# A pairwise bilinear kernel: five equal x tiles in a ring, w first, fewer places ahead, and one more block of x through GpSimd

## The chip, the cores and the metric

The kernel runs on one core of one Trainium2 chip. The metric is the device time of one execution in microseconds (us). All executions that are compared here are in the fast state. One kernel varies by 1 to 5 us from run to run, so the experiments were run in five rounds beside the kernel before on the same chip, and they come with a 95% interval.

## The reference

For every pair i < j of the 32 features of a row, the feature vector x[i] (64 numbers) is multiplied by the pair's own 64 x 64 matrix, and the product is multiplied by x[j] element by element.

```python
def _L0_rec_ref(inputs, W):                      # inputs (4096, 32, 64), W (496, 64, 64)
    idx_i, idx_j = np.triu_indices(F, k=1)       # 496 pairs
    vi = inputs[:, idx_i, :]
    vj = inputs[:, idx_j, :]
    vidots = jnp.einsum('bpd,pde->bpe', vi, W)
    return vidots * vj                           # (4096, 496, 64) float32
```

The output is 520 MB, the inputs are 42 MB. The kernel mainly writes.

## The kernel before

The rows are worked on in 32 tiles of 128 rows, two tiles to a block. For each tile TensorE turns x (a transpose), multiplies by w, and VectorE multiplies the product by x[j] on its way out of PSUM. Some steps (`aside`) go through ScalarE and GpSimd instead. A finished group of pairs, about 4 MB, is stored from one of three buffers in `ob`. The names PE, DVE, ACT, POOL and SP in the profile are TensorE, VectorE, ScalarE, GpSimd and the queue that issues the stores. In the code, `...` marks what is left out; type annotations are left out too.

```python
    LEAD = 3                        # the first three tiles run side by side, group by group
    # ring of five x tiles; blocks in slots 0 and 3 have a gap of 16 numbers between their tiles
    starts = [0, FD + GAP, 2 * FD + GAP, 3 * FD + GAP, 4 * FD + 2 * GAP]
    def slot_of(blk):
        e, second = divmod(blk, 2)
        return ((1, 3), (2, 0))[e % 2][second]

    SWR = 120
    def turn_engines(k):            # a tiny transfer: which engines GpSimd's next transfer begins on
        ...
    def load_fifteen(blk):          # a block of x on GpSimd's queue, for 15 engines of 16
        rows = rows_of(x, blk).rearrange("(p k) f d -> p k f d", k=NB)
        dst = x_block(blk)
        def part(ps, ks):
            tc.keep_in_program_order(nc.gpsimd.dma_start(out=dst[ps, ks], in_=rows[ps, ks]))
        part(slice(0, SWR), slice(0, NB))
        turn_engines(1)
        for k in range(NB):
            part(slice(SWR, P), slice(k, k + 1))
    ...
    AHEAD = 6                       # x is turned so many steps before its first use
    LATE = 4                        # two blocks are loaded in the 5th step of every 4th tile
    loads = {place[2 * NB * e - 1, LATE]: 2 * e for e in range(1, NBLK // 2)}

    load_x(0, nc.sync, 0, 1)        # start: half a block of x, then w
    load_w(0)
    load_w(1)
    ...
    for s, (t, st) in enumerate(sched):
        if s in loads:
            load_fifteen(loads[s] + 1)                          # odd block: GpSimd
        if s - 3 in loads:
            tc.keep_in_program_order(load_x(loads[s - 3], nc.scalar))   # even block: ACT
        ...                                                     # turns, matmuls
        if i in aside and c0 == 0:
            nc.scalar.copy(dst, src)
            nc.gpsimd.tensor_mul(dst, dst, xj)
        else:
            nc.vector.tensor_mul(dst, src, xj)
        if pa + m in ends:
            nc.sync.dma_start(out=..., in_=ot[...])             # store of a group
```

Of the kernel before, what the change touches and what calls it, by code (L numbers as in the profile page):

```python
# [8 lines left out]
F32 = mybir.dt.float32  # L9
# [3 lines left out]
def kernel(  # L13
# [17 lines left out]
    nc = tc.nc  # L31

    B, F, D = x.shape
    P = 128
    NB = 2
    assert 2 * D == P and B % (2 * NB * P) == 0
    NBLK = B // (NB * P)
    NT = NBLK * NB
# [4 lines left out]
    RUN = 8  # L43
# [9 lines left out]
    LEAD = 3  # L53
# [3 lines left out]
    for t in range(NT):  # L57
        b = lead if t < LEAD else later
# [4 lines left out]
    const = ctx.enter_context(tc.tile_pool(name="const", bufs=1))  # L63
# [4 lines left out]

    wT = const.tile([P, NP, E2], F32, tag="wT", name="wT")
    FD = F * D  # L70
    GAP = 16
    xb = const.tile([P, 5 * FD + 3 * GAP], F32, tag="xb", name="xb")
    XT = 2 * (RUN // 2) * P
    xtb = const.tile([P, 2 * XT], F32, tag="xtb", name="xtb")
    ob = const.tile([P, 3 * cap1, D], F32, tag="ob", name="ob")
# [4 lines left out]
    def out_home(n: int, later_: bool):  # L80
        o, c = ((2 - n % 3) * cap1, cap1) if later_ else ((2 - n % 3) * cap0, cap0)
        return ob[:, o : o + c, :]
# [8 lines left out]
    def xt_home(t: int):  # L91
        n = xt_used[0]
        xt_used[0] += 1
        n = n % 4 if t < LEAD else n % 2
        mem, o = (xtb, n * XT) if n < 2 else (xb, (n - 2) * XT)
        return mem[:, o : o + XT].rearrange("p (s u b) -> p s u b", s=2, b=P)





    starts = [0, FD + GAP, 2 * FD + GAP, 3 * FD + GAP, 4 * FD + 2 * GAP]

    def slot_of(blk: int):
        e, second = divmod(blk, 2)
        return ((1, 3), (2, 0))[e % 2][second]

    def tile_of(t: int):

        blk, k = divmod(t, NB)  # L110
        return blk, 1 - k if slot_of(blk) == 0 else k

    def x_block(blk: int):
        o = starts[slot_of(blk)]
        step = starts[slot_of(blk) + 1] - o
        wide = xb[:, o : o + NB * step].rearrange("p (k n) -> p k n", k=NB)
        return wide[:, :, :FD].rearrange("p k (f d) -> p k f d", d=D)

    def x_tile(t: int):
        blk, k = tile_of(t)  # L120
        return x_block(blk)[:, k]

    def rows_of(dram: bass.AP, blk: int) -> bass.AP:
        return dram[blk * NB * P : (blk + 1) * NB * P]

    def load_x(blk: int, eng, k0: int = 0, k1: int = NB):
        src = rows_of(x, blk).rearrange("(p k) f d -> p k f d", k=NB)
        return eng.dma_start(out=x_block(blk)[:, k0:k1], in_=src[:, k0:k1])
# [4 lines left out]
    SWR = 120  # L133
# [4 lines left out]
    def turn_engines(k: int):  # L138
        n = k if k > 1 else 17
        c = used[0] % 8  # L140
        used[0] += 1
        src = x[: NB * n].rearrange("(p k) f d -> p k f d", k=NB)
        tc.keep_in_program_order(
            nc.gpsimd.dma_start(out=scratch[:n, :, c : c + 1], in_=src[:, :, 0, 0:1])  # L144
        )

    def load_fifteen(blk: int):
        rows = rows_of(x, blk).rearrange("(p k) f d -> p k f d", k=NB)
        dst = x_block(blk)

        def part(ps: slice, ks: slice):
            tc.keep_in_program_order(nc.gpsimd.dma_start(out=dst[ps, ks], in_=rows[ps, ks]))  # L152

        part(slice(0, SWR), slice(0, NB))
        turn_engines(1)
        for k in range(NB):
            part(slice(SWR, P), slice(k, k + 1))



# [4 lines left out]
    def raw_w(c: int):  # L165
        if c + 1 < len(wrows):
            a = wrows[c + 1][0]
            return wT[:, a : a + P, :].rearrange("p r e -> p (r e)")
        return ob[:, 3 * cap1 - RAW :, :].rearrange("p r e -> p (r e)")

    def load_w(c: int):
        a = wrows[c][0]
        nc.sync.dma_start(out=raw_w(c), in_=wflat[a : a + P])

    def order_w(c: int, k: int, copy):

        r = wrows[c][1] - wrows[c][0]
        o = k * RP if c == 0 else 3 * cap1 - RAW - (1 + k % 2) * RP
        rp = ob[:, o : o + RP, :].rearrange("p r e -> p (r e)").rearrange("p (e h d) -> p e h d", h=2, d=D)
        src = raw_w(c)[:r].rearrange("p (d h e) -> p e h d", h=2, d=D)  # L180
        ins = copy(rp[:r], src[:, k * EU : (k + 1) * EU])  # L181
        if c > 0:
            tc.keep_in_program_order(ins)
        return rp

    def turn_w(c: int, k: int, rp, copy):
        a, b = wrows[c]
        r = b - a
        pt = psum.tile([P, EU, P], F32, tag="ps", name=f"ptw_{c}_{k}")
        for n in range(EU):  # L190
            nc.tensor.transpose(pt[:, n, :r], rp[:r, n].rearrange("p h d -> p (h d)"), ident[:r, :r])  # L191
        copy(wT[:, a:b, k * EU : (k + 1) * EU], pt[:, :, :r].rearrange("p e r -> p r e"))  # L192

    def turn_x(t: int, q: int, copy):


        pt = psum.tile([P, RUN // 2, P], F32, tag="ps", name=f"ptx_{t}_{q}")
        for u in range(RUN // 2):
            f = q * RUN + 2 * u
            nc.tensor.transpose(pt[:, u, :], x_tile(t)[:, f : f + 2, :].rearrange("p f d -> p (f d)"), ident)  # L200
        xT = xt_home(t)
        copy(xT[:, 0], pt)  # L202
        copy(xT[D:, 1], pt[:D])  # L203
        copy(xT[:D, 1], pt[D:])  # L204
        return xT
# [15 lines left out]
    first = {}  # L221
# [13 lines left out]
    place = {ts: n for n, ts in enumerate(sched)}  # L235


    AHEAD = 6
    due: dict = {}
    for t in range(NT):  # L240
        for q in range(F // RUN):
            at = place[t, first[t, q * RUN]] - AHEAD
            due.setdefault(max(0, at), []).append(("x", t, q))
    for c, orders, turns in (
        (1, (2, 4, 8, 10), (4, 7, 12, 15)),
# [6 lines left out]
    LATE = 4  # L252
    loads = {place[2 * NB * e - 1, LATE]: 2 * e for e in range(1, NBLK // 2)}

    load_x(0, nc.sync, 0, 1)
    load_w(0)
    load_w(1)
    load_x(0, nc.sync, 1, NB)
    load_x(1, nc.sync)
# [3 lines left out]

    v, p, a = nc.vector.tensor_copy, nc.gpsimd.tensor_copy, nc.scalar.copy
    xT, rps = {}, {}
    xT[0, 0] = turn_x(0, 0, a)
    due[0] = [d for d in due[0] if d != ("x", 0, 0)]
    for k, copy in enumerate((v, v, v, a)):
        rps[0, k] = order_w(0, k, copy)
    for k, copy in ((0, a), (3, a), (1, v), (2, a)):  # L270
        turn_w(0, k, rps.pop((0, k)), copy)

    n_out = {}
    for s, (t, st) in enumerate(sched):
        blk, kt = tile_of(t)
        g, i, c0, m = steps[t][st]
        if s in loads:
            load_fifteen(loads[s] + 1)
        if s - 3 in loads:
            tc.keep_in_program_order(load_x(loads[s - 3], nc.scalar))  # L280
        for what, *args in due.get(s, ()):
            if what == "x":
                xT[tuple(args)] = turn_x(*args, a)
            elif what == "turn":
                turn_w(*args, rps.pop(tuple(args)), a)
            else:
                c, k = args
                rps[c, k] = order_w(c, k, ((v, v, p, v), (v, v, p, a))[k % 2][c])

        base, end = groups[t][g]  # L290
        pa = p0[i] + c0
        if pa == base:
            ot = out_home(len(n_out), t >= LEAD)
            n_out[t, g] = ot
        ot = n_out[t, g]
        ps = psum.tile([P, 2, CH, E2], F32, tag="ps", name=f"ps_{s}")
        for h in range(2):
            nc.tensor.matmul(  # L298
                ps[:, h, :m, :],
                xT[t, i // RUN][h * D : (h + 1) * D, (i + h) % 2, i % RUN // 2, :],  # L300
                wT[h * D : (h + 1) * D, pa : pa + m, :],
                start=True,
                stop=True,
            )
        o = pa - base
        j = i + 1 + c0
        dst = ot[:, o : o + m, :].rearrange("p m (h e) -> p m h e", h=2)
        src = ps[:, :, :m, :].rearrange("p h m e -> p m h e")
        xj = x_tile(t)[:, j : j + m, :].rearrange("p m (h e) -> p m h e", h=2)
# [6 lines that stand above are left out]
        ends = (p0[2], end) if (t, g) == (0, 0) else (end,)  # L316
        if pa + m in ends:
            n0 = p0[2] if len(ends) > 1 and pa + m == end else base
            nc.sync.dma_start(
                out=rows_of(out, blk).rearrange("(p k) n d -> p k n d", k=NB)[:, kt, n0 : pa + m, :],  # L320
                in_=ot[:, n0 - base : pa + m - base, :],
            )
# [28 lines left out]
```

## Time and profile before

| | before |
|---|---|
| time | 1334.1 us (median of 3 runs) |
| profiled span | 1333.2 us |
| busy: PE, DVE, ACT, POOL | 86%, 71%, 35%, 42% |
| moved by DMA | 563.16 MB, 422 GB/s over the span |

A row of the page's second part has 40 slices of the span; a digit is a busy share in tenths. In a line of the waits the first engine waits and the one behind the arrow is what it waited for. In a line of the windows come the times, then busy time (and instructions) of PE, PEld, DVE, ACT and POOL, the granted clock, the DMA share and GB/s. A DMA share of 1.00 means that all 16 engines had packets in hand, and 0.06 that one had. A share of 1.00 at a low rate means packets that take longer than usual.

### The profile page before, as it was taken

The numbers are of one execution on the slowest core, as the hardware profiler recorded it, in microseconds if no ns is written. First come the engines' busy times: TensorE is split into PE (matmuls) and PEld (weight loads), VectorE is DVE, ScalarE is ACT, GpSimd is POOL, SyncE is SP. The second block draws the span as 40 slices with busy tenths as digits, with TensorE's granted clock in tenths as the row PEclk, the third lists the DMA queues.
The fourth block names the chain that finished last, engine by engine and source line by source line (L and its number), as shares of the span: only waits on it lengthen the run. The fifth ranks groups of instructions, "written<-read, shape, count | busy, mean of one in ns | idle before, by whom it ended". The sixth has DMA issues, their size and how long they took to land.

```text
span 1333.2 us, 17377 instructions
## 1 busy us (share of the span) xinstructions
PE 1146.3 (86%) x6644; PEld 597.9 (45%) x6644; DVE 952.0 (71%) x1287; ACT 471.6 (35%) x627; POOL 558.5 (42%) x264
## 2 busy tenths in 40 slices
PE   6989989996989979998888888888888988888983
PEld 3555444443444434444444444444444444444441
DVE  5778767875777757777667776777767776677773
ACT  4553423333333323333233332343333332333330
POOL 1862524435434434344344352444434444334440
PEclk9999989998999989999899998999989999899997
DMA  9999999999999999999999999999999999999997
GB/s 389 431 430 429 381 428 433 429 433 422 428 431 434 426 423 431 430 431 428 420 435 428 434 411 426 428 433 430 422 425 437 424 430 403 428 433 430 424 426 307
DMA packets 24306, 563.16 MB, mean 422 GB/s; under 512 B 3232, under 2 KB 3232, under 8 KB 3360
## 3 DMA queue, kind: packets, MB, share of 16 engines
q1 hardware_dynamic: 20576, 532.69, 93.5%
q0 software_dynamic: 2640, 14.70, 2.8%
q10 hardware_dynamic: 1008, 14.68, 2.8%
q8 instruction: 52, 0.85, 0.2%
q14 instruction: 30, 0.25, 0.0%
HBM read 41.94 MB, written 520.09 MB: 422 GB/s over the span
## 4 chain that ended last, share of the span: by engine, by line
DMA 48%; PE 25%; DVE 11%; issue 8%; POOL 4%; ACT 3%; DVEq 0%; SPq 0%; ACTq 0%; POOLq 0%
DMA out_dram<-ob 47%; PE ps L298 22%; DVE ob L314 11%; POOL ob L312 3%; ACT ob L311 2%; PE ptx L200 2%; DMA xb<-in_r_inputs_dram 1%; PE ptw L191 1%; POOL xb L152 0%; DVE ob L181 0%; POOL scratch L144 0%; POOL ob L181 0%; DVEq L314 0%; ACT xtb L202 0%; ACT xtb L204 0%
## 5 line engine op out<-in xcount | busy, mean ns | idle before, releaser
L314 DVE TENSOR_TENSOR ob<-ps,xb 128x1024 f32<-128x1024 f32 (+4 forms) x1277 | 939.8, 793 | 347.9 <-DMA out_dram<-ob 173.8
L298 PE MATMUL ps<-wT,xtb 64*128 64x512 f32 (+15 forms) x5760 | 1015.4, 490 | 145.9 <-DVE ob L314 72.5
L312 POOL TENSOR_TENSOR ob<-ob,xb 128x1024 f32<-128x1024 f32 x224 | 529.1, 2367 | 744.6 <-ACT ob L311 717.3
L298 PEld LDWEIGHTS ps<-wT,xtb 64*128 64x128 f32 x5760 | 507.6, 195 | 619.2 <-DVE ob L314 257.1
L311 ACT COPY ob<-ps 128x1024 f32<-128x1024 f32 x224 | 226.8, 1013 | 485.9 <-PE ps L298 342.5
L202 ACT COPY xtb<-ptx 128x512 f32<-128x512 f32 x122 | 71.5, 586 | 311.4 <-PE ptx L200 309.7
L200 PE MATMUL ptx<-ident,xb 128*128 128x128 f32 x512 | 86.2, 292 | 10.8 <-DMA xb<-in_r_inputs_dram 7.1
L200 PEld LDWEIGHTS ptx<-ident,xb 128*128 128x128 f32 x512 | 55.1, 144 | 61.9 <-issue 37.5
L204 ACT COPY xtb<-ptx 64x512 f32<-64x512 f32 x122 | 71.0, 582 | 3.0
L203 ACT COPY xtb<-ptx 64x512 f32<-64x512 f32 x122 | 70.4, 577 | 2.9
L298 PE MATMUL ps<-wT,xb 64*128 64x512 f32 (+15 forms) x244 | 42.5, 465 | 3.4 <-DVE ob L314 1.6
L298 PEld LDWEIGHTS ps<-wT,xb 64*128 64x128 f32 x244 | 20.2, 185 | 21.3 <-DVE ob L314 9.4
L191 PE MATMUL ptw<-ident,ob 128*128 128x128 f32 (+1 forms) x128 | 18.1, 294 | 6.0 <-DVE ob L181 5.8
L191 PEld LDWEIGHTS ptw<-ident,ob 128*128 128x128 f32 (+1 forms) x128 | 15.1, 154 | 12.0 <-DVE ob L181 5.2
L192 ACT COPY wT<-ptw 128x1024 f32<-128x1024 f32 (+1 forms) x15 | 14.9, 992 | 10.1 <-PE ptw L191 10.0
L181 DVE COPY ob<-wT 128x1024 f32<-128x1024 f32 (+1 forms) x7 | 9.5, 1382 | 10.5 <-DMA wT<-in_L_rec_W_dram 10.5
L152 POOL DMA_DIRECT2D xb<-in_r_inputs_dram x21 | 13.3, 636 | 0.0
L202 ACT COPY xb<-ptx 128x512 f32<-128x512 f32 x6 | 3.5, 586 | 18.1 <-PE ptx L200 18.1
L144 POOL DMA_DIRECT2D scratch<-in_r_inputs_dram x9 | 8.4, 934 | 0.3 <-issue 0.3
L181 POOL COPY ob<-wT 128x1024 f32<-128x1024 f32 x4 | 8.0, 2004 | 0.0
L181 ACT COPY ob<-ob 128x1024 f32<-128x1024 f32 x2 | 4.1, 2028 | 0.0
L204 ACT COPY xb<-ptx 64x512 f32<-64x512 f32 x6 | 3.5, 583 | 0.1
(11 smaller groups left out, 11.3 us busy)
## 6 DMA issues: line engine op xcount, KB each, us to landing
out_dram<-ob SPq DMA_DIRECT2D x29, 4064.0 KB, 19.5
out_dram<-ob SPq DMA_DIRECT2D x29, 4032.0 KB, 19.9
out_dram<-ob SPq DMA_DIRECT2D x29, 4000.0 KB, 19.8
out_dram<-ob SPq DMA_DIRECT2D x29, 3776.0 KB, 20.2
xb<-in_r_inputs_dram ACTq DMA_DIRECT2D x7, 2048.0 KB, 22.5
xb<-in_r_inputs_dram POOLq DMA_DIRECT2D x7, 1920.0 KB, 33.7
out_dram<-ob SPq DMA_DIRECT2D x3, 2912.0 KB, 12.6
out_dram<-ob SPq DMA_DIRECT2D x3, 2624.0 KB, 11.2
```

Of the source, the lines that this page charges most:

```text
L152: tc.keep_in_program_order(nc.gpsimd.dma_start(out=dst[ps, ks], in_=rows[ps, ks]))
L181: ins = copy(rp[:r], src[:, k * EU : (k + 1) * EU])
L191: nc.tensor.transpose(pt[:, n, :r], rp[:r, n].rearrange("p h d -> p (h d)"), ident[:r, :r])
L192: copy(wT[:, a:b, k * EU : (k + 1) * EU], pt[:, :, :r].rearrange("p e r -> p r e"))
L200: nc.tensor.transpose(pt[:, u, :], x_tile(t)[:, f : f + 2, :].rearrange("p f d -> p (f d)"), ident)
L202: copy(xT[:, 0], pt)
L203: copy(xT[D:, 1], pt[:D])
L204: copy(xT[:D, 1], pt[D:])
L298: nc.tensor.matmul(ps[:, h, :m, :], xT[t, i // RUN][h * D : (h + 1) * D, (i + h) % 2, i % RUN // 2, :], wT[h * D : (h + 1) * D, pa : pa + ...
L311: nc.scalar.copy(dst, src)
L312: nc.gpsimd.tensor_mul(dst, dst, xj)
L314: nc.vector.tensor_mul(dst, src, xj)
```

## The change

The intent was to make the five tiles of the ring equal (no gap) and put the two tiles of a GpSimd block into places that don't touch; to have w's first part and the first matmuls sooner; and to give block 14, too, to GpSimd, whose loads leave one DMA engine out.

```diff
-    GAP = 16
-    xb = const.tile([P, 5 * FD + 3 * GAP], F32, tag="xb", name="xb")
+    xb = const.tile([P, 5, FD], F32, tag="xb", name="xb")
...
+    fifteen = (3, 5, 7, 9, 11, 13, 14, 15)
+    def slots_of(blk: int):
         e, second = divmod(blk, 2)
-        return ((1, 3), (2, 0))[e % 2][second]
+        if e == 0:
+            return ((1, 2), (3, 4))[second]
+        if e % 2 == 0:
+            return ((2, 3), (1, 4))[second]
+        if 2 * e in fifteen:
+            return ((1, 3), (2, 0))[second]
+        return ((1, 2), (3, 0))[second]
...
-        part(slice(0, SWR), slice(0, NB))
+        part(slice(0, SWR), slice(0, F))
         turn_engines(1)
-        for k in range(NB):
-            part(slice(SWR, P), slice(k, k + 1))
+        for h in range(2):
+            part(slice(SWR, P), slice(h * F // 2, (h + 1) * F // 2))
...
-    AHEAD = 6
+    AHEAD = {t: 4 if t < LEAD else 6 for t in range(NT)}
...
+    load_w(0)
     load_x(0, nc.sync, 0, 1)
-    load_w(0)
...
-    xT[0, 0] = turn_x(0, 0, a)              # now after two of the four turns of w
...
         if s in loads:
-            load_fifteen(loads[s] + 1)
-        if s - 3 in loads:
+            for b in (loads[s], loads[s] + 1):
+                if b in fifteen:
+                    load_fifteen(b)
+        if s - 3 in loads and loads[s - 3] not in fifteen:
```

The last 8 rows of a GpSimd block thus come in halves by features (16 pieces of 4 KB each) and no longer by tiles (8 pieces of 8 KB each).

More of the change, by code (lines that the diff above doesn't have):

```diff
@@ L94, in xt_home @@
         n = n % 4 if t < LEAD else n % 2
-        mem, o = (xtb, n * XT) if n < 2 else (xb, (n - 2) * XT)
+        mem, o = (xtb, n * XT) if n < 2 else (xb[:, 0], (n - 2) * XT)
         return mem[:, o : o + XT].rearrange("p (s u b) -> p s u b", s=2, b=P)
-    starts = [0, FD + GAP, 2 * FD + GAP, 3 * FD + GAP, 4 * FD + 2 * GAP]
-    def slot_of(blk: int):
+    fifteen = (3, 5, 7, 9, 11, 13, 14, 15)
+    def slots_of(blk: int):
         e, second = divmod(blk, 2)
-        return ((1, 3), (2, 0))[e % 2][second]
+        if e == 0:
[5 more added lines that the diff above has]
+        return ((1, 2), (3, 0))[second]
     def tile_of(t: int):
         blk, k = divmod(t, NB)
-        return blk, 1 - k if slot_of(blk) == 0 else k
+        a, b = slots_of(blk)
+        return blk, k if a < b else 1 - k
     def x_block(blk: int):
-        o = starts[slot_of(blk)]
-        step = starts[slot_of(blk) + 1] - o
-        wide = xb[:, o : o + NB * step].rearrange("p (k n) -> p k n", k=NB)
-        return wide[:, :, :FD].rearrange("p k (f d) -> p k f d", d=D)
+        a, b = sorted(slots_of(blk))
+        return xb[:, a : b + 1 : b - a].rearrange("p k (f d) -> p k f d", d=D)
     def x_tile(t: int):
@@ L149, in load_fifteen, with part @@
         dst = x_block(blk)
-        def part(ps: slice, ks: slice):
-            tc.keep_in_program_order(nc.gpsimd.dma_start(out=dst[ps, ks], in_=rows[ps, ks]))
-        part(slice(0, SWR), slice(0, NB))
+        def part(ps: slice, fs: slice):
+            tc.keep_in_program_order(nc.gpsimd.dma_start(out=dst[ps, :, fs], in_=rows[ps, :, fs]))
+        part(slice(0, SWR), slice(0, F))
         turn_engines(1)
-        for k in range(NB):
-            part(slice(SWR, P), slice(k, k + 1))
+        for h in range(2):
+            part(slice(SWR, P), slice(h * F // 2, (h + 1) * F // 2))
     wflat = w.rearrange("p d e -> p (d e)")
@@ L241 @@
         for q in range(F // RUN):
-            at = place[t, first[t, q * RUN]] - AHEAD
+            at = place[t, first[t, q * RUN]] - AHEAD[t]
             due.setdefault(max(0, at), []).append(("x", t, q))
@@ L271 @@
         turn_w(0, k, rps.pop((0, k)), copy)
+        if k == 3:
+            xT[0, 0] = turn_x(0, 0, a)
     n_out = {}
```

## The prediction

> **What bounds the kernel now.** I read four things in this order: the rates by slice and the queues on the page, windows of two microseconds at the end, the waits, and the timeline around one load of x.
>
> The page first: the mean busy share of the 16 DMA engines in 40 slices, what they moved, and the queues.
> ```profile
> DMA  9999999999999999999999999999999999999997
> GB/s 389 431 430 429 381 428 433 429 433 422 428 431 434 426 423 431 430 431 428 420 435 428 434 411 426 428 433 430 422 425 437 424 430 403 428 433 430 424 426 307
> ...
> q1 hardware_dynamic: 20576, 532.69, 93.5%
> q0 software_dynamic: 2640, 14.70, 2.8%
> q10 hardware_dynamic: 1008, 14.68, 2.8%
> q8 instruction: 52, 0.85, 0.2%
> ```
> The engines are busy nearly all the time and the rate has a plateau at 428 to 437 GB/s. The kernel is DMA-bound: the queues' shares add to 99.3%. PE (86%) and DVE (71%) follow. So shortening a chain of arithmetic pays only where a DMA engine would have had nothing to do. The rate is low in four places: the first slice (2 us before the first packet), slice 5 (381), the slices with a load of x (403 and 411 the worst) and the last (307).
>
> The last slice, in windows of 2 us. The last two columns are DMA share and GB/s; nothing computes any more.
> ```profile
> 1322.00:1324.00 2.00, 0.00 (x0) 0.00 (x0) 0.00 (x0) 0.00 (x0) 0.00 (x0) 0.50 0.75 323
> 1324.00:1326.00 2.00, 0.00 (x0) 0.00 (x0) 0.00 (x0) 0.00 (x0) 0.00 (x0) 0.50 0.08 32
> 1326.00:1328.00 2.00, 0.00 (x0) 0.00 (x0) 0.00 (x0) 0.00 (x0) 0.00 (x0) 0.50 0.04 16
> 1328.00:1330.00 2.00, 0.00 (x0) 0.00 (x0) 0.00 (x0) 0.00 (x0) 0.00 (x0) 0.50 0.07 32
> ```
> A share of about 1/16 means that one engine is still working, 8 us after the rest. The trace also holds each transfer's 16 landing times, one per engine. For the last store they are 1323.89 (first), 1323.99 (8th), 1325.4 (15th) and 1332.13 (last). **One DMA engine, always behind, sets the end.** The distance from 8th to last is 1.3 us for the store issued at 313.16, after two loads of x, and grows to 8.1 for the last store before the load at 790 and to 9.1 before that at 1116. After these two loads it is 2.6 and 4.7, then it grows to 8.15 at the end.
>
> Why it lags: queue 8 (instructions) has 52 packets of 16 KB. In the trace one comes about every 25 us, they never overlap, and they take 950 ns on average: 49.5 us. I infer that they are all on this engine; the trace doesn't name engines. Why the lag drops: GpSimd's loads give 120 rows to 15 engines and leave one out.
>
> Now the waits: first the store queue's own, then DVE's on a buffer of ob.
> ```profile
> SPq L319 <- DVE ob L314: 1133.9, 135, 19.3
> ```
> ```profile
> DVE ob L314 <- DMA out_dram<-ob: 173.8, 77, 8.2
> ```
> The store queue waits for DVE with two stores usually outstanding (19.5 us to landing, about 9.4 us each), so this costs nothing while the queue is stocked. DVE's wait is for the slow engine: a buffer is free only when its last engine has landed.
>
> Last the start, in windows of the columns PE, PEld, DVE, ACT, POOL, clock, share, GB/s.
> ```profile
> 120.00:138.00 18.00, 17.34 (x128) 10.22 (x124) 15.74 (x30) 4.77 (x9) 0.00 (x0) 1.00 0.99 423
> 138.00:156.00 18.00, 17.93 (x110) 9.63 (x110) 15.77 (x22) 7.29 (x9) 12.77 (x9) 1.00 0.98 354
> 156.00:172.00 16.00, 9.59 (x60) 4.83 (x56) 6.96 (x12) 5.52 (x8) 6.47 (x3) 0.90 1.00 418
> ```
> Until 156 us PE is 96 to 100% busy and just fails to keep the queue stocked: the store issued at 139.49 came as its predecessor's first share landed (139.48); the next, at 150.46, came after the first landing of that one (147.94), and its first packets ran only at 155. Against 432 GB/s, 138 to 156 lost (432 - 354) x 18 / 432 = 3.3 us.
>
> **What the Trainium skill says.** "DMA: Bandwidth & Descriptors", section "Where 436 GB/s comes from", gives a ceiling of 435 GB/s for 16 ports. The trace agrees: a store packet of 32512 B takes 1204 ns, 27.0 GB/s, or 432 on 16. Its section "Why a DMA increments its semaphore by 16 and not by 1" says that all 16 engines must report, and that GpSimd's transfers on fewer engines go to consecutive ones from a rotating cursor. The first agrees with the landing times above; the second fits the falls of the lag but no view names an engine. Section "Queues, rings and completion order" says that an engine takes its queues in turn, a packet each. The trace agrees: beside stores of 30 KB packets GpSimd's 8 KB ones move about 92 GB/s (321 to 330 us).
>
> **The change part by part.**
>
> *Block 14 moves from ACT to GpSimd.* On ACT's queue the slow engine gets 8 packets of 16 KB, 8 x 611 = 4.89 us. Of GpSimd's load it gets 1 packet of 8 KB, 0.31 us. It saves 4.58 us. The 15 others go from 4.89 to 17 x 309 ns = 5.25 us, +0.36 each. During the load at 1116 the slow engine's landings of two successive stores are 1121.48 and 1135.87, 14.4 us apart, which is just 8 store packets of 1.194 us and 4.89 us of x: it ran without a hole, so the saving comes through whole: its end moves from 1332.13 to 1327.55, and the others' last from 1325.4 to 1325.8. It remains last.
>
> What that load costs on GpSimd: issuing one block took 0.83 + 1.01 + 1.07 = 2.91 us, and it sits between two multiplies that the first store of that tile needs:
> ```profile
> 1116.53 0.83 POOL L152 DMA_DIRECT2D xb<-in_r_inputs_dram  x1
> 1117.36 1.01 POOL L144 DMA_DIRECT2D scratch<-in_r_inputs_dram  x1
> ...
> 1118.36 1.07 POOL L152 DMA_DIRECT2D xb<-in_r_inputs_dram  x2
> ...
> 1119.44 2.36 POOL L312 TENSOR_TENSOR ob<-ob,xb 128x1024 f32<-128x1024 f32 x1
> ```
> Its store went out at 1121.83. With two blocks it goes 2.9 us later. For 15 engines that is a longer time without stores, but they have 3.9 MB of GpSimd's loads to do then; the slow one has stores left until about 1131. Block 14 then moves at 92 GB/s instead of sharing with ACT: first packet some 4.7 us after issue, 1.97 MB / 92 = 21.4 us, and about 2.2 us for each of three small transfers behind. It is whole at about 1149, against 1139 on ACT. Tile 28 was first turned at 1153. This just fits.
>
> *w first.* 1 MB of x took 2.45 us of the queue (first share of w landed 4.9 us after it for 2 MB), so w lands at 8.0 instead of 10.5. The w turns end some 2 us earlier with the x turn among them. *Four places ahead.* Tile 1's turn stood before the first matmul of tile 0 and waited for x until 17.86; now two steps (about 1 us of PE each) go before it. Together PE's work from 18 to 156 us moves forward by about 2 us. The loads already fill the DMA until 33, so nothing is gained there; at 138 to 156 the stores come 2 us sooner. The slow engine took 18.2 us from 152.07 to 170.29 for some 13.4 us of packets, so part of these 2 us is also its own. I choose 1.2.
>
> *Five equal tiles, blocks apart, halves by features.* GpSimd's odd blocks were already in 8 KB packets (a gap of 64 B kept them apart). The same packets go to other tiles; the two small parts become 4 KB pieces in the same number of bytes. Block 1 gets 16 KB packets in place of 8 KB: 16 x 309 - 8 x 611 = 0.06 us. Zero.
>
> Sum: 1334.1 - 4.6 - 1.2 = 1328.3; a little for the later store at 1125: 1328.5.
>
> **Rivals.** (a) The loads take longer, not shorter. GpSimd's queue alone with 3.9 MB could hold tile 28 past 1153. For: the small transfers land 2.2 us apart. Against: the queue holds one to two stores (9.4 us each). If it stalls by over 8 us: 1332 to 1336. (b) The 15 others become the bound, because the later store starves them: they have only 1.8 us of room. A hole of 3 us makes 1329 to 1330. (c) The new places interleave two blocks, so the program might take the strided ranges as overlapping and make ACT's load wait for GpSimd's (34 us to landing) six times. For: ACT works in order, so its copies would stall behind. Against: the strides describe disjoint tiles. It would be 1360 or more. (d) The start gains all of 3.3 us for all engines: 1326. (e) The spared engine is not the slow one: then -0.8, 1333. The falls of the lag speak against it.
>
> **Range and chances.** Nearly all ways lie within 0.7% of before; the bytes don't change. The largest gain that I can make of the tail and the start is 8 us, 0.6%; 2% would be 27 us. Only (c) makes over 2% slower. Range 1325 to 1333.
>
> **What would show it.** Right: the last store's last landing is some 3 us behind its 8th instead of 8.1; one fewer ACT load of x and 2 more small GpSimd transfers; the first store goes out 1.5 to 3 us before 25.24; slice 5 is above 390 GB/s; the mean rate rises from 422 to 424 GB/s (563.16 MB in some 1327.6 us). Wrong: the tail still ends with one engine alone for 8 us; waits on x appear in PE's list beyond the 7.1 us at the start; or ACT's x loads are issued tens of microseconds after GpSimd's.

## The result, and the profile after

The changed kernel took 1330.03 us (median of 4 runs, 1329.89 to 1332.44), the kernel before beside it 1334.9 us (4 runs). The ratio is 0.9966 (0.9949 to 0.9984). A ratio here is the mean time of one kernel's fast runs over that of the other's of the same rounds, so it isn't quite the ratio of the medians. The profiled span is 1328.1 us.

First the page after, its rates by slice and its queues:

```profile
GB/s 388 432 429 432 384 429 434 430 431 424 431 429 435 431 412 432 430 430 431 422 432 427 431 417 419 434 429 432 414 427 431 430 431 382 419 432 431 430 431 387
...
q1 hardware_dynamic: 20448, 532.69, 93.8%
q0 software_dynamic: 3264, 16.80, 3.5%
q10 hardware_dynamic: 864, 12.58, 2.4%
q8 instruction: 52, 0.85, 0.2%
```

One block of 2.1 MB has gone from queue 10 (ACT) to queue 0 (GpSimd). The last slice has 387 GB/s instead of 307. Slice 5 (133 to 166 us) has hardly moved, 384 against 381. And a new low has come up: 382 in slice 34, where block 14 is loaded, against 403.

The end after, in windows of 2 us:

```profile
1320.00:1322.00 2.00, 0.00 (x0) 0.00 (x0) 0.00 (x0) 0.00 (x0) 0.00 (x0) 0.50 0.90 387
1322.00:1324.00 2.00, 0.00 (x0) 0.00 (x0) 0.00 (x0) 0.00 (x0) 0.00 (x0) 0.50 0.97 419
1324.00:1326.00 2.00, 0.00 (x0) 0.00 (x0) 0.00 (x0) 0.00 (x0) 0.00 (x0) 0.50 0.38 161
1326.00:1328.00 2.00, 0.00 (x0) 0.00 (x0) 0.00 (x0) 0.00 (x0) 0.00 (x0) 0.50 0.00 0
```

The 6.8 us in which one engine worked alone (from the 15th landing at 1325.38 to the last at 1332.13) are gone: all 16 end within 3 us. But the others now work at full share until 1324, later than before. The 16 landing times of a store, which the trace holds without the engines' names, show both (in us):

```
store                    kernel     first     8th      15th     last
issued 1101.3 / 1100.6   before    1112.25  1112.38  1116.28  1121.48
                         after     1111.52  1112.40  1114.44  1120.19
(load of blocks 14, 15)
issued 1147.6 / 1141.2   before    1161.72  1162.64  1164.48  1167.33
                         after     1159.60  1164.82  1165.25  1165.99
the last store           before    1323.89  1323.99  1325.38  1332.13
                         after     1324.10  1325.54  1326.59  1326.95
```

In front of that load the last landing comes 1.3 us earlier than before, and the 8th at the same time. Behind it the last landing is one of the crowd, and the 8th comes 2.2 us later than before. In the changed kernel it is the *first* landing that moves: 5.2 us ahead of the 8th after the load, 1.1 us ahead in the store issued at 1271. That is the movement which the *last* one makes before (4.7 us behind the 8th after the load, 8.1 at the end).

The packets show that it is the same engine. Each of the 8 packets that a store gives an engine starts within 6 ns of the end of the one before, so an engine's work can be followed by its times. In the kernel before, the 40 packets from 1263.7 to 1312.5 us that lead to the last landing took 44 ns more, on the mean, than the least for their size; the other engines' packets in that time took 8 ns more. Packets of 32000 B, for instance, took 1213 to 1265 ns on it and 1189 (median) on the others. In the changed kernel the engine with this mark is the first to land at 1159.60. It then falls back into the crowd and is fifth in the last store, at 1324.97. So it lost its place as last, and led at first.

What happened in the load. GpSimd's timeline after, which answers to the one that the prediction shows:

```profile
1113.53 2.36 POOL L319 TENSOR_TENSOR ob<-ob,xb 128x1024 f32<-128x1024 f32 x1 [12.97 <-ACT ob L318]
1115.83 0.79 POOL L156 DMA_DIRECT2D xb<-in_r_inputs_dram  x1
1116.61 0.98 POOL L148 DMA_DIRECT2D scratch<-in_r_inputs_dram  x1
1117.59 1.86 POOL L156 DMA_DIRECT2D xb<-in_r_inputs_dram  x3
1119.45 0.96 POOL L148 DMA_DIRECT2D scratch<-in_r_inputs_dram  x1
1120.41 1.10 POOL L156 DMA_DIRECT2D xb<-in_r_inputs_dram  x2
1121.54 6.99 POOL L319 TENSOR_TENSOR ob<-ob,xb 128x1024 f32<-128x1024 f32 x3
```

GpSimd issues for 5.7 us, and only then come the multiplies for which the store of this tile waits; it goes out at 1123.93, and 1121.83 before. The windows of this stretch, before and then after:

```profile
1110.00:1120.00 10.00, 9.96 (x56) 4.76 (x54) 7.05 (x10) 3.01 (x4) 5.75 (x6) 1.00 1.01 424
1120.00:1130.00 10.00, 7.11 (x32) 3.77 (x34) 6.18 (x7) 2.79 (x4) 5.23 (x3) 0.83 0.97 352
```
```profile
1110.00:1120.00 10.00, 9.26 (x48) 4.21 (x44) 6.35 (x7) 3.69 (x5) 6.47 (x7) 1.00 1.06 436
1120.00:1130.00 10.00, 7.29 (x44) 3.99 (x44) 7.13 (x8) 2.10 (x3) 8.50 (x6) 1.00 0.94 253
```

For ten microseconds the rate is 253 GB/s at a share of 0.94: the 15 engines have almost only GpSimd's loads, and these packets of 8 KB take longer (a median of 614 ns) than the 309 ns that they need elsewhere.

The start. DVE's and ACT's waits for a buffer of `ob` between 24 and 66 us, before and then after:

```profile
ACT ob L311 <- DMA out_dram<-ob: 2.6, 2, 2.1
...
DVE ob L314 <- DMA out_dram<-ob: 1.7, 1, 1.7
```
```profile
DVE ob L321 <- DMA out_dram<-ob: 8.7, 3, 4.1
...
ACT ob L318 <- DMA out_dram<-ob: 5.8, 2, 3.0
```

The first matmul on w begins at 17.13 instead of 18.56 us and the third store goes out at 34.18 instead of 37.05. But then the engines wait 14.5 us for buffers instead of 4.3, and by the eleventh store (85.27 against 85.57) the lead is 0.3 us.

### The profile page after: what moved, and what is told of

Same layout as the page of the kernel before. It is cut to its first block, busy times and chain, and to the rows that moved or that the text cites. A ratio compares the mean times of both kernels' runs of the same rounds, so it can differ in the third digit from the quotient of the medians.

```text
span 1328.1 us, 17383 instructions
## 1 busy us (share of the span) xinstructions
PE 1142.9 (86%) x6644; PEld 599.4 (45%) x6644; DVE 950.6 (72%) x1287; ACT 471.1 (35%) x627; POOL 561.5 (42%) x268
## 4 chain that ended last, share of the span: by engine, by line
DMA 49%; PE 22%; DVE 11%; issue 9%; POOL 4%; ACT 3%; DVEq 0%; ACTq 0%; SPq 0%; POOLq 0%
DMA out_dram<-ob 48%; PE ps L305 20%; DVE ob L321 10%; POOL ob L319 3%; ACT ob L318 3%; PE ptx L204 2%; DMA xb<-in_r_inputs_dram 1%; POOL xb L156 0%; ACT xtb L206 0%; ACT xtb L208 0%; ACT xtb L207 0%; DVE ob L185 0%; PE ptw L195 0%; POOL ob L185 0%; ACT ob L185 0%
```

## The experiments

| run | what it is | us (median) | ratio to before, 95% |
|---|---|---|---|
| changed kernel | | 1330.03 | 0.9966 (0.9949 to 0.9984) |
| e1_act14 | changed, block 14 on ACT | 1333.34 | 0.9986 (0.9979 to 0.9992) |
| e2_old_start | changed, old start | 1330.76 | 0.9959 (0.9946 to 0.9971) |
| e3_before_whole | before, blocks 13 and 15 on all 16 engines | 1339.86 | 1.0033 (1.0021 to 1.0045) |
| e4_after_whole15 | changed, block 15 on all 16 engines | 1332.40 | 0.9971 (0.9960 to 0.9983) |
| e5_start_only | before with the new start | 1335.58 | 1.0000 (0.9992 to 1.0008) |
| e6_ring_only | before with ring and halves | 1333.62 | 0.9986 (0.9979 to 0.9993) |
| e7_late8 | changed, loads 4 steps later | 1330.78 | 0.9962 (0.9950 to 0.9975) |
| e8_before_late8 | before, loads 4 steps later | 1336.40 | 1.0007 (0.9999 to 1.0015) |
| e9_before_halves | before with the halves alone | 1397.40 | 1.0464 (1.0450 to 1.0477) |
| e10_late1 | changed, loads 3 steps earlier | 1328.57 | 0.9949 (0.9937 to 0.9961) |
| e11_split15 | changed, block 15's load 4 steps behind 14's | 1331.46 | 0.9972 (0.9961 to 0.9982) |
| e12_ring_parts | before with the ring alone | 1335.03 | 0.9998 (0.9990 to 1.0006) |

The kernel before had medians of 1334.98 to 1335.77 us beside them. All gave correct results.

### e1_act14: block 14 back on ACT

```diff
-    fifteen = (3, 5, 7, 9, 11, 13, 14, 15)
+    fifteen = (3, 5, 7, 9, 11, 13, 15)
```

> The changed kernel with block 14 back on ACT's queue (start, ring and halves as changed). Theory A (the whole gain is the eighth GpSimd load; the start and the ring give nothing): the time of before within 1.5 us, 1333 to 1335.5, one engine alone for 7 to 8 us at the end, about 8 us between 8th and last landing of the last store. Theory B (the start is worth 1 us or more, as predicted): 1332 to 1333. Theory C (most of the gain is from start and ring): 1331 or less.

Measured: 0.9986, 1.9 us under before. In the profile the last store's landings are 1322.29 (8th) and 1330.08 (last): the last landing nearly 8 us behind the 8th again, and one engine alone for 6.2 us (the 15th landed at 1323.93). So the eighth GpSimd load removes the lonely end. The time lies at the edge of theory A's band, 1.9 us below before by the ratio, which theory A did not allow for: something else in the change gives 1.9 us, and block 14 gives the rest. The next runs look for both.

### e2_old_start and e5_start_only: the start taken out, and alone

```diff
-    AHEAD = {t: 4 if t < LEAD else 6 for t in range(NT)}
+    AHEAD = {t: 6 for t in range(NT)}
...
-    load_w(0)
     load_x(0, nc.sync, 0, 1)
+    load_w(0)
...                                         # and the turn of tile 0 back in front of w's
```

> The changed kernel with the start of before (x in front of w, tile 1 turned before the first matmul, six places ahead everywhere). Theory A (start worth nothing): the time of the changed kernel, 1329.5 to 1331, and the window 138 to 156 us at 350 to 356 GB/s as in both. Theory B (the start is worth 1 us or more): 1331 to 1333, and less than 350 GB/s there.

e5 is the kernel before with the same edit the other way round.

> The kernel before with the start of the change alone (first part of w in front of x, tile 1 turned after two steps, four places ahead in the first three tiles). Theory A (the start gives nothing, since the loads fill the DMA until 33 us and the stores' buffers hold the pace from 66 to 123 us): the time of before within 1 us, and the rate from 138 to 156 us within 5 GB/s of 354. Theory B (the start gave the 1.9 us by which the kernel with block 14 back on ACT beat before): 1.5 to 2.5 us faster than before.

Measured: without the new start the changed kernel takes 1330.76 us, 0.9959, with 350 GB/s at 138 to 156 us; the start alone gives a ratio of 1.0000, with an interval of 1.1 us on either side, and e5 has 357 GB/s at 138 to 156 us. Theory A holds in both. No gain of the start can be seen.

### e6_ring_only, e12_ring_parts and e9_before_halves: where 1.9 us come from

e6 is e1 and e2 together: of the change only the ring and the halves are left.

> The changed kernel with the start of before and block 14 on ACT, so of the change only the ring of five equal tiles and the halves by features are left. Theory A (the 1.9 us come from these): 1.5 to 2.5 us faster than before. Theory B (they come from the start): within 1 us of before.

Measured: 0.9986, just as e1. So the 1.9 us belong to ring and halves together. e9 puts the halves alone into the kernel before:

```diff
-        part(slice(0, SWR), slice(0, NB))
+        part(slice(0, SWR), slice(0, F))
         turn_engines(1)
-        for k in range(NB):
-            part(slice(SWR, P), slice(k, k + 1))
+        for h in range(2):
+            part(slice(SWR, P), slice(h * F // 2, (h + 1) * F // 2))
```

> The kernel before with one edit: the last 8 rows of a GpSimd block come in two halves by features (16 pieces of 4 KB each) instead of two halves by tile (8 pieces of 8 KB each). Theory A (the 1.9 us of ring and halves together come from the halves): 1.5 to 2.5 us faster than before. Theory B (they come from the ring's places): within 1 us of before.

Measured: 1397.4 us, 4.6% slower, which neither theory has. What GpSimd waited for in e9:

```profile
POOL xb L152 <- DMA xb<-in_r_inputs_dram: 108.9, 4, 29.1
POOL xb L152 <- DVE ob L314: 86.1, 3, 29.1
```

In each of the seven loads GpSimd stands for some 28 us (195 us in all) before it issues the second half. GpSimd's timeline of one load in e9:

```profile
312.91 2.35 POOL L312 TENSOR_TENSOR ob<-ob,xb 128x1024 f32<-128x1024 f32 x1
344.32 0.58 POOL L152 DMA_DIRECT2D xb<-in_r_inputs_dram  x1 [29.06 <-DVE ob L314]
344.92 6.99 POOL L312 TENSOR_TENSOR ob<-ob,xb 128x1024 f32<-128x1024 f32 x3
```

Everything behind it in GpSimd's order, the multiplies too, comes 29 us late, and the stores stop: 222 GB/s at a share of 0.57 in the window 336 to 346. What it waits for is the landing of the first half: the last landing of that one is at 343.70, and in all seven loads the second half goes out 0.3 to 0.6 us after it. (The lines above put three of these waits down to DVE, which by the landing times was not the reason.) The two halves write different features, so neither needs the other. The program orders them as if they overlapped where the two tiles of a block are a gap apart; how its tracking of overlaps comes to that was not looked into. In the ring of equal tiles there is no such wait. e12 is the converse, the ring with the old cut by tiles:

> The ring of five equal tiles alone: the changed kernel with the start of before, block 14 on ACT, and the last 8 rows of a GpSimd block in two halves by tile as before (8 pieces of 8 KB each). Theory A (the 1.9 us come from the halves by features, 0.27 us a load): the time of before within 0.8 us, and the kernel with the halves besides is 1.5 us or more faster. Theory B (they come from the ring's places): 1.5 to 2.5 us faster than before, as with the halves.

Measured: 0.9998. Theory A holds, if narrowly (the intervals of e6 and e12 just touch, and e1 stands with e6): the ring alone gives nothing, ring and halves give 1.9 us, and the halves can't be had without the ring. Why they help stays open. The bytes are the same. Nor is it 0.27 us in each of seven loads, as the expectation has it: in e12 and e6 the last landings are 0.3 us apart in front of the last load (1121.10 and 1121.37) and 1.7 us behind it (1157.41 and 1155.74), in one profile of each. The kernel before goes with e12 there (1157.41), e1 with e6 (1155.29).

### e3_before_whole and e4_after_whole15: is the engine left out the one that sets the end?

```diff
-            load_fifteen(loads[s] + 1)
+            if loads[s] + 1 in (13, 15):
+                tc.keep_in_program_order(load_x(loads[s] + 1, nc.gpsimd))   # 128 rows at once
+            else:
+                load_fifteen(loads[s] + 1)
```

> The kernel before with blocks 13 and 15 loaded by GpSimd on all 128 rows at once, so that no engine is left out in these two loads (16 packets of 8 KB on each engine instead of 17 on fifteen and 1 on one). Theory A (the engine left out is the one that lags and sets the end): it gets 2 x 15 packets of 309 ns more, 9.3 us; the end moves to 1342 to 1345, 8th to last landing of the last store 16 to 19 us. Rival (another engine lags, or the lag is not from work on it): the time of before within 2 us, and 8 to 9 us between 8th and last.

The end of e3 in windows of 2 us:

```profile
1326.00:1328.00 2.00, 0.00 (x0) 0.00 (x0) 0.00 (x0) 0.00 (x0) 0.00 (x0) 0.50 1.20 516
1328.00:1330.00 2.00, 0.00 (x0) 0.00 (x0) 0.00 (x0) 0.00 (x0) 0.00 (x0) 0.50 0.12 48
1330.00:1332.00 2.00, 0.00 (x0) 0.00 (x0) 0.00 (x0) 0.00 (x0) 0.00 (x0) 0.50 0.08 32
1332.00:1334.00 2.00, 0.00 (x0) 0.00 (x0) 0.00 (x0) 0.00 (x0) 0.00 (x0) 0.50 0.07 32
1334.00:1336.00 2.00, 0.00 (x0) 0.00 (x0) 0.00 (x0) 0.00 (x0) 0.00 (x0) 0.50 0.04 16
```

Measured: 1339.86 us, 4.4 us more than before by the ratio. The direction is theory A's and the rival (no effect) falls, but the size is half. Two things can be read. The last landing of the last store is 1336.62, and the 8th 1328.92: the distance is 7.7 us, not 16 to 19. The other engines came later too. A likely reason is that a store can only be issued when the slowest engine has emptied a buffer, so that a lag much over one store's length (9.4 us) makes the others wait; no run tests it. And the load left out also leaves out the tiny transfer of `turn_engines`, so the edit takes something away as well. In the stretch of the load at 957, four successive last landings are 47.5 us apart in sum before and 49.1 us in e3, 1.6 us for a load and not 4.6. How this divides is left open.

```diff
-                if b in fifteen:
+                if b == 15:
+                    tc.keep_in_program_order(load_x(b, nc.gpsimd))
+                elif b in fifteen:
                     load_fifteen(b)
```

> The changed kernel with block 15 loaded on all 128 rows at once (block 14 still leaves one engine out). Theory A (in the changed kernel the spared engine comes first, 2.9 us before the last one): it gets 4.6 us more and comes out last by little, the others 0.36 us less; the end moves by +1 to +2, 1331 to 1332. Rival (the spared engine is still the last one): +4.6, 1334 to 1335. Rival 2 (the engine is not concerned): 0 to -0.5.

Measured: 1332.40 us, 2.4 us over the changed kernel's median (0.0005 by the ratios, whose intervals overlap; the two were not run in one call). In the profile the last store's landings are 1324.58 (8th), 1325.54 (15th) and 1329.49 (last), and the last one falls behind step by step, as before. Theory A fits: with one load less to its favour the engine with the slow packets is last again, with two it is among the first. From 1324.97 (fifth, changed kernel) to 1329.49 (last, here) it is 4.5 us, near the 4.6 us for which the load was meant. The rival, +4.6 us on the time, would have had this engine last in the changed kernel.

### e7_late8 and e8_before_late8: the loads four steps later

```diff
-    LATE = 4
+    LATE = 8
```

> The changed kernel with the loads of x four steps later in their tile, behind GpSimd's second multiply of the first store. Theory A (in the changed kernel the other 15 engines are the bound, and they lose time where GpSimd's issues hold the first store back): the store during the last load goes out about 5 us sooner (1118 to 1119), the excess at 1120 to 1130 falls below 2 us, 138 to 156 us above 370 GB/s, and the time falls by 1.5 to 4 us to 1326 to 1328.5. Rival (the spared engine is the bound, or the loads now come too late for the next tile): 1330 or more.

The windows of e7, at the start and in the last load:

```profile
138.00:156.00 18.00, 17.91 (x106) 9.54 (x108) 15.47 (x19) 6.80 (x8) 12.74 (x9) 1.00 0.89 346
...
1120.00:1130.00 10.00, 9.41 (x48) 4.92 (x46) 7.37 (x10) 2.03 (x2) 8.21 (x7) 0.83 0.99 409
```

Measured: 1330.78 us, no gain. Half of theory A came true: the store in the last load goes out at 1117.11 instead of 1123.93, and the hole there is filled, 409 GB/s instead of 253. But at 138 to 156 us the rate is 346 GB/s at a share of 0.89. There the loads of x had filled the time in which the stores run dry, and four steps later they no longer do. And block 14 comes too late. What PE waited for between 1140 and 1160 us in e7:

```profile
PE ptx L204 <- DMA xb<-in_r_inputs_dram: 5.4, 1, 5.4
```

One hole was traded for two smaller ones.

> The kernel before with the loads of x four steps later in their tile. Theory A (one lagging engine sets the end, and it has stores left while the others starve): the holes get smaller for the others but the time stays within 1 us of before, and the distance from 8th to last landing of the last store grows to 9 us or more or the others wait longer for buffers. Rival (holes cost every engine alike): 2 to 4 us faster than before, like the changed kernel with the same edit.

Measured: 1336.4 us, 1.0007. It is within 1 us of before, as theory A had it, and the distance from 8th to last is 7.8 us, not 9 or more. Since the same edit makes a hole at 138 to 156 us here too (338 GB/s), this run doesn't separate "holes don't matter for the engine that is last" from "a hole filled and a hole made". It is inconclusive.

### e10_late1: the loads three steps earlier

```diff
-    LATE = 4
+    LATE = 1
```

> The changed kernel with the loads of x three steps earlier in their tile, before GpSimd's first multiply. Theory A (in the changed kernel the hole at 1120 to 1130, 253 GB/s, costs the 15 other engines 2 to 3 us, and block 14 must not come later): the store during the last load goes out at about 1120 instead of 1123.9, block 14 is whole before 1146, 1120 to 1130 above 320 GB/s; the time falls by 1 to 2.5 us to 1327.5 to 1329. Rival (no gain: another hole or the spared engine takes its place): 1329.5 or more.

```profile
138.00:156.00 18.00, 17.64 (x102) 9.32 (x104) 15.58 (x19) 6.81 (x8) 12.78 (x9) 1.00 0.97 369
...
1120.00:1130.00 10.00, 9.98 (x52) 5.42 (x50) 7.29 (x10) 2.67 (x3) 4.36 (x3) 0.79 1.00 418
```

Measured: 1328.57 us (1328.24 to 1329.05), 0.9949, the fastest of all. GpSimd issues the loads before the first multiply of the tile (1106.92 to 1112.6) and both multiplies follow at once, so the store goes out at 1117.32. The loads are early enough to fill the time at 138 to 156 us (369 GB/s against 353 after) and for tile 28. Theory A holds here. But the gain over the changed kernel, 1.5 us by the medians, isn't clear of the noise by the ratios, whose intervals overlap; the two were not run in one call. The last store's landings are 1319.07 (first), 1321.72 (8th), 1324.67 (15th) and 1326.12 (last): the engine with the slow packets is last again, alone for 1.5 us. A further load through GpSimd might pay now; it was not tried.

### e11_split15: block 15's load behind the multiply

```diff
         if s in loads:
-            for b in (loads[s], loads[s] + 1):
-                if b in fifteen:
-                    load_fifteen(b)
+            load_fifteen(loads[s] if loads[s] in fifteen else loads[s] + 1)
+        if s - 4 in loads and loads[s - 4] in fifteen:
+            load_fifteen(loads[s - 4] + 1)
```

> The changed kernel with block 15's load four steps behind block 14's, so that GpSimd's multiply goes between the two. Theory A: GpSimd holds the store back by 2.9 instead of 5.8 us, it goes out at about 1121, block 14 comes as in the changed kernel (whole at about 1148), 1120 to 1130 above 300 GB/s; the time falls by 0.5 to 2 us to 1328 to 1329.5. Rival: no change (1329.5 to 1331), because the hole comes from the reads of x themselves and not from the late store.

Measured: 1331.46 us, no gain. The store goes out 5.3 us after the load begins instead of 8.1, and the window 1120 to 1130 has 308 GB/s instead of 253, as theory A had it. But the last landing is 1328.85, with the 8th at 1325.25. The last one has the slow packets and falls back from the crowd, as the lagging engine does. So the smaller hole was not what the time hung on in this form; what made the lagging engine later was not found.

## Why the prediction was right or wrong

**The time.** 1328.5 was forecast with 1325 to 1333; 1330.03 was measured. The class, within 2%, was as forecast. Parts of the sum were wrong and partly made up for each other, so that it came out close is in part luck. Of the signs named, the mean rate came true (424 GB/s). The last landing was 1.4 us behind the 8th and not 3, slice 5 stayed at 384 GB/s, and the first store came later. The parts:

| part | predicted | measured |
|---|---|---|
| block 14 through GpSimd | -4.6 us | -2.7 us (0.9966 against 0.9986), or -3.6 (e2 against e1, on one chip) |
| start (w first, four ahead) | -1.2 us | 0.0 us (e5) |
| ring, blocks apart, halves | 0 | -1.9 us (e6), by the halves on the ring (e12 without them: 0.9998) |
| later store in the last load | +0.2 us | contained in the first row |

**What bounds the kernel: right. Why one engine lags: wrong.** DMA bounds it, and one lagging engine set its end. Taking its load away removed the lonely end (the windows after), and giving load back made the end later (e3, e4). But the prediction put the lag down to the 52 instruction packets, and the trace speaks against that. The instruction packets at 1275.73 and 1302.12 us fall in the time in which the lagging engine can be followed, and its store packets run through both without a gap. They ran on other engines, where the next store packet took 400 ns longer. What the lagging engine has is slower packets, 44 ns each, until about the time of the last store's issue (1312.80). What slows them isn't in the trace and stays open. The forecast didn't rest on this reason, only on the lag.

**"The saving comes through whole ... It remains last": wrong.** This is the step that failed. The engine did gain: from the last landing at 1121.48 to 1147.03 it took 25.6 us for two stores before, and from 1120.19 to 1139.50 (now as the first) 19.3 us after, 6.2 us less where 4.58 was forecast. (In e1, with the new halves and block 14 on ACT, it took 24.6 us, 5.3 more than after.) But it came out in front. The end passed to the other 15 engines, and they landed at 1326.95, where 1325.8 was forecast. This is rival (b), which was given 1.8 us of room. Its cause was named but put too low: GpSimd issued for 5.7 us, the store went out at 1123.93 (1124.7 forecast), and for ten microseconds the rate was 253 GB/s. "They have 3.9 MB of GpSimd's loads to do then" was the mistake: with these loads almost alone, the 15 engines did not run at full rate. Over 1120 to 1130, packets took longer than their usual time by 3.4 us on the mean engine, against 1.5 before. e10 shows that this hole can be had away, with 418 GB/s there. Its time is lower, though it mends 138 to 156 us as well. e11, which fills half of the hole, has no gain, so what the hole alone costs is not shown.

**Block 14 "just fits": right.** It was whole at 1148.3 (about 1149 forecast), and tile 28 was turned at 1149.3 without a wait for it. In e7, a little later, the wait was there. Rival (a) did not come about.

**The start: wrong.** "PE's work moves forward by about 2 us" held only at first. The step that failed is that the lead would last until 138 us. Between 24 and 66 us the lead turned into waits for the buffers of `ob` (14.5 us against 4.3); by the eleventh store 0.3 us of it was left, and 138 to 156 us had 353 GB/s against 354. Nor did the first store come sooner (25.81 against 25.24): it waits for GpSimd's multiply, and in ACT's order the copy in front of that multiply stands behind the three copies of tile 1's turn.

**"Five equal tiles, blocks apart, halves by features ... Zero": wrong by 1.9 us.** Counting bytes and packets did not show what the cut of the last 8 rows does to the end; in the traces the gain comes at the last load. And the ring had a purpose that I had not seen: without it the halves make GpSimd wait 195 us and cost 62 us (e9). The zero for the time of the ring alone was right (e12).

**Rivals (c), (d) and (e).** No load waited falsely for another in the changed kernel, so (c) falls. Such a wait does appear where the halves meet the old ring (e9). The start gained nothing, so (d) falls. The engine left out is the lagging one (e3, e4, and the slow packets), so (e) falls.

## What to carry to other kernels

Where DMA bounds a kernel, look at the landing times of single engines as well as at the mean share: work taken from the last engine pays only until the next ones are last, and what one does to those others (here a store held back behind the issuing of loads) has to be worked out as carefully. An issuing engine that also computes should issue its loads where nothing waits for its next result: moving them three steps took the store of that tile from 1123.93 to 1117.32 us here, and the kernel's time down by 1.5 us by the medians, which isn't clear of the noise. A lead at the beginning is lost again where a ring of buffers sets the pace soon after: the new start gave nothing.

## What the Trainium skill lacked or had wrong

- "DMA: Bandwidth & Descriptors", section "Latency and other measured facts", says that engines 7 and 15 are usually slower and guesses at the descriptor rings of GpSimd's transfers. Here one engine (the trace doesn't say which) had slower packets, by 43 ns of some 1200 on the mean, from 1263.7 to 1303 us too, when no packet of GpSimd's queue ran. So these transfers are not the reason in that stretch. Leaving this engine out of one more load took away an end of 6.8 us in which it worked alone.
- The same section puts the first byte at about 1 us for GpSimd's transfers and 0.6 us for the others. With stores in flight the first packets of GpSimd's load at 1116 came 4.5 us after its issue in both kernels, and those of the store issued at 150.46 (before) at 155.58.
- The same page, section "Anatomy of one DMA — SWDGE (gpsimd) path", gives some 50 ns for dispatch and calls descriptor generation small. In these traces GpSimd is held for 0.53 to 1.0 us by each transfer that it issues, 2.9 us for the four of one block. Nothing there says that this lies in the way of GpSimd's own arithmetic.
- No page tells how the last 8 rows of a block are best cut: two halves of 16 pieces of 4 KB gave a time 1.6 us lower (0.9986 against 0.9998 of before, e6 and e12) than two of 8 pieces of 8 KB, with the same bytes. The cause is open.
